# Experts' first block begun in attention's last steps, its weights in eight pieces, and GpSimd in a written order

## The chip, the cores and the metric

The kernel runs on one core of a Trainium2 chip. Its engines are named as the profile names them: PE (TensorE, with PEld for loading weights into it), DVE (VectorE), ACT (ScalarE), POOL (GpSimd) and SP (SyncE); "SPq" and "POOLq" are the DMA queues that SP and GpSimd issue to. The metric is the device time of one execution in microseconds, lower is better. One execution was also profiled; its time and its trace are what lines and intervals are read from.

## The reference

Four images of 32 x 32 tokens with 384 channels go through two layers in 32-bit floats. The part that matters here is the first layer:

```python
# --- layer 0 (metaformer) ---
x = x + _L0_conv_ref(_ln_c(x), ...)      # attention, 12 heads of 32 channels
t = _to_tokens(x)
t = t + _L0_ffn_ref(_ln_t(t), ...)       # four experts, each token goes to two
...
attn = softmax(einsum('bhnd,bhmd->bhnm', q, k) * scale)
attn = attn * final                       # final: row weights x column weights, from groups and a top 96
attn = attn / (attn.sum(axis=2, keepdims=True) + 1e-08)
out = einsum('bhnm,bhmd->bhnd', attn, v)
return out @ proj_w.T
...
scores = einsum('bsd,de->bse', x, gate_w) + gate_b
topk_vals, topk_idx = top_k(softmax(scores), 2)
h = gelu(einsum('bsd,edh->ebsh', x, w1) + b1, approximate=False)
y = einsum('ebsh,ehd->ebsd', h, w2) + b2
out = einsum('bse,ebsd->bsd', masked, y)
```

So each of 1024 tokens per image attends to all the others, column sums of the weighted attention are needed before the values are summed up, and each token is then worked on by the two experts with its highest gate values. The second layer (an outlook attention over 3 x 3 neighbourhoods and a dense layer from a Kronecker product) follows and is not touched.

## The kernel before

**Attention** (`attention`, line 177) runs one main loop (line 882 on) over 202 steps: 4 images x 12 heads = 48 heads, four steps (u = 0 to 3) to a head, two 128-token tiles of keys to a step, and ten more steps at the end in which the last head drains. The variable `step` counts from 0; steps from 192 on have no scores left. In one step, in this order: the scores of the head (PE, line 649) and their exponentials (ACT, line 659); `out`, the weighted values of eight steps before (PE, line 667, into `ps_o`); the softmax's row sums of one step before (PE, line 667, into `ps_z`). At u = 0 the row sums of the head before are gathered (ACT, then SP through a row in DRAM, `z_row`, and back as `zz`), and the next head's `Head` is made: eight small DMAs on GpSimd's queue (lines 636 and 637) that spread its q and k over the partitions. At u = 3 the head that is complete is kept (line 731 on): ACT copies it from PSUM, and SP and GpSimd put it in its place (`q<-po`, GpSimd's two add to what is there). DVE takes the steps `share` of seven steps before (line 711, two passes over 128x1024, then small ones to line 718), at u = 1 `spread` (lines 693 to 699, through `r_row` in DRAM and back as `rz`, broadcast to all partitions), and the preparation of the next image's groups and masks.

The tail of an image lies in the steps of the next: projection and residual (line 766), and then its routing (`routed`, line 793, and `Router`, line 1241), a generator from which the loop takes one portion per step. Routing computes gates and top two on DVE, gives every token a slot in its expert's list, and writes the list to a table in DRAM with 16 scatters per image on GpSimd's queue (line 1400). When the third image's routing is complete, `Router.first` (line 1408) fixes the experts of the first four blocks. It does so before the fourth image's tokens are known; they fill later blocks. The fourth image's projection and routing are done within the experts (`left`, called there `beside`).

**Experts** (`experts`, line 1573) works on 35 blocks of one expert and 256 tokens each: n = 0 to 3 from the first three images, n = 4 to 6 of 128 tokens only, and n = 7 to 34 from all. For a block, GpSimd's queue loads the expert's two weight matrices by an indirect DMA each (`up`, 128x4620 floats, 2.37 MB, and `down`, 128x4992 floats, 2.56 MB, line 1603), the block's slots of the table (`ids`, line 1617) and its tokens (`xb`, line 1627). DVE normalizes the tokens (`norm`, line 1636), PE transposes them (`turn`, line 1646), then twelve `up` chunks of 128 hidden units, six matmuls each (line 1723), with a gelu on ACT (line 1728), then the `down` matmuls: plain ones in blocks 0 and 4 to 6 (line 1747), a form with fewer products and more sums in the others (lines 1767 to 1774). The results go to DRAM by SP (`yg<-y`). In block 0 a portion of `beside` follows each of six chunks. The weights have two buffers (`halves`), so weights of block n+1 are loaded while block n is worked on, each as soon as block n-1 has read it for the last time. When both experts of a tile of 128 tokens have been there, `add` (line 1650) loads the tile's residual `x` by SP, gathers its two results (`yt`, GpSimd, line 1567), adds them (DVE, line 1658) and stores (SP). In the second half of the blocks one tile is added per block.

**Order.** For PE, DVE, ACT and SP the instructions stand in the order in which the program issues them (`tc.manual_schedule`). GpSimd's are placed by the framework's scheduler in this kernel, so that they may run ahead of the program's order, as far as their buffers allow.

Of the kernel before, what the change touches and what calls it, by code (L numbers as in the profile page):

```python
# [10 lines left out]
FP = mybir.dt.float32  # L11
# [165 lines left out]
def attention(net, outer, router, x, x1, unsafe, qkv_wT, gpT, proj_wT, proj_w, gate_w, gate_b):  # L177
# [24 lines left out]
    with ExitStack() as ctx:  # L202

        early = ctx.enter_context(tc.tile_pool(name="at_early", bufs=1))
# [664 lines left out]

        step = -100  # L870
# [18 lines left out]
        for step in range(STEPS + OUT + 2):  # L889
# [13 lines left out]
            if 0 <= step - OUT < STEPS:  # L903
                if (step - OUT) % PAIRS == PAIRS - 1:
                    heads[(step - OUT) // PAIRS].keep()
            b, i = divmod(step, PAIRS * NH)
# [9 lines left out]
            if b and o > 2 * NB:  # L916
                next(routing[b - 1], None)
# [15 lines left out]
            search()  # L933
        residue(B - 1, 0)
# [29 lines left out]
    return left  # L964
# [276 lines left out]
class Router:  # L1241
# [10 lines left out]
    def __init__(self, net, pool, keep, psum):  # L1252
# [34 lines left out]
        self.all = None  # L1287
# [11 lines left out]
        self.weight = [keep.tile([P, NT], FP, name=f"weight_{n}", tag=f"weight_{n}") for n in range(2)]  # L1299
        none = const("none", [P, self.LINE], mybir.dt.int32)  # L1300
# [12 lines left out]
    def route(self, b, logit, mean, rs):  # L1313
# [82 lines left out]
        for t in range(NB):  # L1396
            if t % 2 == 0:
                yield
            for n in range(2):
                s = nc.gpsimd.indirect_dma_start(  # L1400
# [172 lines left out]
def experts(net, router, x1, x2, wup, wdown, beside):  # L1573
# [12 lines left out]
    with ExitStack() as ctx:  # L1586
# [4 lines left out]
        halves = [pool(f"ex_{n}", 1) for n in range(2)]  # L1591
# [3 lines left out]
        def rows(n):  # L1595
            w, t = router.firsts if n < NFIRST else router.all
            return w[:, n : n + 1], t[:, n : n + 1]

        def weights(n):
            up = halves[n % 2].tile([P, KC * HID + NF], FP, name="up", tag="up")  # L1600
            down = halves[n % 2].tile([P, NF * C + C], FP, name="down", tag="down")
            for t, w in ((up, wup), (down, wdown)):
                nc.gpsimd.indirect_dma_start(
                    out=t, out_offset=None, in_=w,
                    in_offset=bass.IndirectOffsetOnAxis(ap=rows(n)[0], axis=0),
                )
            return up, down

        beside = beside(work)
        ids, xbs = {}, {}  # L1610

        def tiles(n):
            return 1 if NFIRST <= n < NLEAD else TT

        def tokens(n):
            t = ids[n] = halves[0].tile([P, TT, router.LINE], I32, name="ids", tag="ids", bufs=6)
            nc.gpsimd.indirect_dma_start(
                out=t[:, : tiles(n), :].rearrange("p t w -> p (t w)"), out_offset=None,
                in_=net.table.rearrange("(r t) w -> r (t w)", t=tiles(n)),
                in_offset=bass.IndirectOffsetOnAxis(ap=rows(n)[1], axis=0),  # L1620
            )

        def fetch(n):
            xb = xbs[n] = halves[n % 2].tile([P, TT, C], FP, name="xb", tag="xb")
            last = (B - 1 if n < NFIRST else B) * NTOK
            for t in range(tiles(n)):
                nc.gpsimd.indirect_dma_start(
                    out=xb[:, t, :], out_offset=None, in_=x1[:last, :],
                    in_offset=bass.IndirectOffsetOnAxis(ap=ids[n][:, t, 0:1], axis=0),
                )  # L1630

        def norm(n):
            xb = xbs[n]
            own = ids.pop(n).bitcast(FP)
            for t in range(tiles(n)):
                nc.vector.tensor_scalar(
                    xb[:, t, :], xb[:, t, :], own[:, t, 1:2], own[:, t, 2:3], ALU.subtract, ALU.mult
                )

        def turn(n):  # L1640
            xb = xbs.pop(n)
            xbT = halves[n % 2].tile([P, KC, XB], FP, name="xbT", tag="xbT")
            for t in range(tiles(n)):
                ps = router.psum()
                for c in range(KC):
                    nc.tensor.transpose(ps[:, c * P : (c + 1) * P], xb[:, t, c * P : (c + 1) * P], net.ident)
                nc.vector.tensor_copy(  # L1647
                    xbT[:, :, t * P : (t + 1) * P], ps[:, :C].rearrange("p (c t) -> p c t", c=KC)
                )
            return xbT  # L1650
# [39 lines left out]
        ws = {0: weights(0)}  # L1690
        for n in range(NFIRST):
            tokens(n)
        fetch(0)
        norm(0)
        xbT = turn(0)
        for n in range(NXB):
# [6 lines left out]
            if n + 1 < NXB:  # L1703
                if n + 1 >= NFIRST:
                    tokens(n + 1)
                ws[n + 1] = weights(n + 1)
                fetch(n + 1)
# [5 lines left out]
            up, down = ws.pop(n)  # L1713
# [5 lines left out]
            for f in (*range(0, 3), *range(6, 9), *range(3, 6), *range(9, 12)):  # L1719
                ps = ps_h.tile([P, XB], FP, name="ps_h", tag="h")[:, :size]  # L1720
                for k in range(KC):
                    o = k * HID + f * P
                    nc.tensor.matmul(  # L1723
                        ps, lhsT=up[:, o : o + P], rhs=xbT[:, k, :size], start=k == 0, stop=k == KC - 1,
                    )
# [57 lines left out]
            if n + 1 < NXB:  # L1783
                xbT = turn(n + 1)
# [684 lines left out]
```

## Time and profile before

| | |
|---|---|
| time, three runs | 2757.79, 2760.5, 2776.32 us; median 2760.5 |
| profiled execution | 2739.55 us; its span 2737.4 us, mean TensorE clock 0.964 |
| busy over the span | PE 2541.4, DVE 1746.2, ACT 1270.0, POOL 635.3 us |
| start to step 0 and the steps of attention | to about 1196 us |
| experts, blocks 0 to 3 | 1198 to 1348 us |
| half blocks, 4 to 6 | 1348 to 1397 us |
| blocks 7 to 34 | 1397 to 2240 us, 29.84 us for an undisturbed one |
| second layer | 2242 to 2737 us |

Busy times are of the profiled execution. In the window lists each engine's busy time is followed by its count of instructions, then the mean granted TensorE clock, the busy share of the core's 16 DMA engines and the rate. In a timeline a line starts with the time from the span's beginning and the duration; what stands in brackets is the idle time of the engine ahead of it and what ended that. `up<-in_wup_dram` means that the tile `up` is written from the DRAM tensor.

### The profile page before, as it was taken

What the parts mean: (1) busy time and instruction counts of PE and PEld (TensorE: products, weight loads), DVE (VectorE), ACT (ScalarE), POOL (GpSimd) and SP (SyncE); (2) the same over time, 40 slices, a digit from 0 to 9 for tenths busy, and PEclk for the clock granted to TensorE, in tenths of its full rate; (3) what the DMA queues carried; (4) which work ended last, traced back from release to release, by engine and by line L of the source; (5) the groups of instructions that cost most, each with busy time, mean ns of one, the idle gap of its engine ahead of it and who ended that gap; (6) DMA issues with size and microseconds to landing.
All of it is one profiled execution on the core that took longest, in us unless ns stands there. A gap on an engine that the chain in (4) does not pass through costs nothing. (4 is left out here: it accounts for less than half of the span.)

```text
span 2737.4 us, 40223 instructions
## 1 busy us (share of the span) xinstructions
PE 2541.4 (93%) x14667; PEld 1549.7 (57%) x14667; DVE 1746.2 (64%) x4490; ACT 1270.0 (46%) x2086; POOL 635.3 (23%) x909
## 2 busy tenths in 40 slices
PE   6979998989899998779999999999999999999988
PEld 3323332333233332248889999999899984555532
DVE  2367768777788778756434454554555468888962
ACT  3768876768677876512122112112111223545455
POOL 2112322252225222613221112222222121210000
PEclk9989999999999998979999999999999999999989
DMA  5133434422332233444574554666566546765532
GB/s 110 38 98 90 105 92 120 106 61 62 83 89 62 62 98 77 138 153 166 214 279 172 202 214 180 219 220 220 197 219 218 213 139 198 224 209 174 181 108 94
DMA packets 189631, 404.14 MB, mean 148 GB/s; under 512 B 83664, under 2 KB 149520, under 8 KB 176368
## 3 DMA queue, kind: packets, MB, share of 16 engines
q0 software_dynamic: 40784, 238.96, 26.5%
q1 hardware_dynamic: 142064, 156.33, 18.3%
q10 hardware_dynamic: 6576, 6.19, 0.8%
q8 instruction: 118, 1.93, 0.3%
q14 instruction: 89, 0.73, 0.1%
HBM read 304.34 MB, written 49.00 MB: 129 GB/s over the span
## 5 line engine op out<-in xcount | busy, mean ns | idle before, releaser
L1728 ACT ACTIVATE h<-ps_h,up 128x256 f32<-128x256 f32 (+1 forms) x420 | 194.8, 464 | 832.2 <-PE ps_h L1723 829.7
L1723 PE MATMUL ps_h<-xbT,up 128*128 128x256 f32 (+1 forms) x2520 | 530.8, 371 | 0.7 <-DVE xbT L1647 0.7
L1723 PEld LDWEIGHTS ps_h<-xbT,up 128*128 128x128 f32 x2520 | 463.3, 191 | 61.7 <-DVE xbT L1647 1.1
L711 DVE CUSTOM_DVE_ANT_0 e<-e,rz,inv 128x1024 f32<-128x1024 f32 x384 | 475.5, 1275 | 17.6 <-DMA rz<-r_row 17.5
L659 ACT ACTIVATE e<-ps_s,ten 128x1024 f32<-128x1024 f32 x384 | 407.1, 1107 | 62.0 <-PE ps_o L667 32.7
L649 PE MATMUL ps_s<-q,k 32*128 32x512 f32 x1536 | 274.3, 663 | 29.1 <-ACT e L659 28.7
L667 PE MATMUL ps_o<-e,wv 128*32 128x512 f32 x1536 | 227.1, 666 | 69.1 <-DVE wv L718 43.9
L636 POOL DMA_DIRECT2D q<-q x192 | 98.2, 512 | 627.9 <-PE ps_s L649 570.5
L667 PE MATMUL ps_z<-e,rt_ones 128*32 128x512 f32 x1536 | 218.8, 642 | 0.0
L391 ACT ACTIVATE below<-tk_left,tk_bound 128x1024 bf16<-128x1024 f32 (+1 forms) x160 | 184.2, 1151 | 63.5 <-DVE tk_bound L397 52.8
L1767 PE MATMUL ps_y<-wsum,hsum 128*128 128x192 f32 x1116 | 197.9, 331 | 10.1 <-DVE hsum L1683 5.9
L1767 PEld LDWEIGHTS ps_y<-wsum,hsum 128*128 128x128 f32 x1116 | 183.7, 192 | 14.3 <-DVE y L1771 7.7
L649 PEld LDWEIGHTS ps_s<-q,k 32*128 32x128 f32 x1536 | 83.0, 188 | 159.6 <-ACT e L659 90.5
L1907 PE MATMUL ps_a<-wa,xnT 128*128 128x486 f32 x384 | 162.3, 572 | 1.8 <-ACT xnT L174 1.8
L1771 DVE TENSOR_TENSOR y<-ps_y,y 128x192 f32<-128x192 f32 x155 | 55.4, 358 | 167.9 <-PE ps_y L1767 164.8
L667 PEld LDWEIGHTS ps_o<-e,wv 128*32 128x32 f32 x1536 | 32.1, 112 | 228.8 <-issue 94.2
L1567 POOL DMA_INDIRECT yt<-yg,index x64 | 78.8, 1232 | 311.4 <-DVE x L1870 148.9
L306 PE MATMUL ps_t<-xnT,wqkv 128*128 128x512 f32 x288 | 136.4, 615 | 3.3 <-ACT xnT L488 2.6
L637 POOL DMA_DIRECT2D k<-k x192 | 126.1, 657 | 9.2 <-issue 6.0
L667 PEld LDWEIGHTS ps_z<-e,rt_ones 128*32 128x32 f32 x1536 | 53.3, 118 | 131.1 <-issue 129.1
L1767 PE MATMUL ps_y<-down,h 128*128 128x192 f32 x744 | 126.0, 326 | 0.0
L1767 PEld LDWEIGHTS ps_y<-down,h 128*128 128x128 f32 x744 | 122.6, 190 | 1.6
(405 smaller groups left out, 3751.1 us busy)
## 6 DMA issues: line engine op xcount, KB each, us to landing
band<-room SPq DMA_DIRECT2D x32, 1560.0 KB
rz<-r_row SPq DMA_DIRECT2D x48, 512.0 KB
yg<-y SPq DMA_DIRECT2D x67, 192.0 KB
q<-q POOLq DMA_DIRECT2D x192, 64.0 KB, 1.9
k<-k POOLq DMA_DIRECT2D x192, 64.0 KB, 2.0
room<-none SPq DMA_DIRECT2D x64, 192.0 KB
x<-x SPq DMA_DIRECT2D x34, 192.0 KB
o<-in_x_dram SPq DMA_DIRECT2D x33, 192.0 KB
```

The costliest lines, as they stand in the source:

```text
L306: nc.tensor.matmul(ps, lhsT=lhsT(k), rhs=rhs(k), start=k == 0, stop=k == KC - 1)
L391: nc.scalar.activation(junk[:n], left[:n], AF.Sign, bias=bound[:n], accum_out=over[:n])
L636: nc.gpsimd.dma_start(out=self.q4[rows_, :], in_=q[:, 512 * half : 512 * half + 512])
L637: nc.gpsimd.dma_start(out=self.k4[rows_, :].rearrange("p (a t) -> p a t", t=P), in_=k[:, :, odd, :])
L649: nc.tensor.matmul(ps[:, half * 512 : half * 512 + 512], lhsT=self.k4[r, u * P : (u + 1) * P], rhs=self.q4[r, :], start=True, stop=True,)
L659: nc.scalar.activation(e, ps, AF.Exp, bias=shift, scale=QK_SCALE)
L667: nc.tensor.matmul(ps[r : r + 32, :], lhsT=lhsT(odd), rhs=self.es[2 * u + odd][:, half * 512 : half * 512 + 512], start=u == 0, stop=u == ...
L711: nc.vector.tensor_tensor_reduce(self.es[m], self.es[m], self.rz, 1.0, self.im["inv"][:, m, self.h : self.h + 1], ALU.mult, ALU.add, self. ...
L1723: nc.tensor.matmul(ps, lhsT=up[:, o : o + P], rhs=xbT[:, k, :size], start=k == 0, stop=k == KC - 1,)
L1728: nc.scalar.activation(hs[f // 3][:, f % 3, :size], ps, AF.Gelu, bias=up[:, KC * HID + f : KC * HID + f + 1])
L1767: nc.tensor.matmul(ps, lhsT=left[f], rhs=right[:, f, :], start=f == 0, stop=f == HF - 1)
L1907: nc.tensor.matmul(pa[:, :HW_], lhsT=xnTs[i][:, k, :], rhs=wa[:, k, hh * HW_ : (hh + 1) * HW_], start=k == 0, stop=k == KC - 1,)
```

## The change

GpSimd is added to the engines whose order is the program's. What the scheduler did is thereby replaced by the order of the calls: in experts, for block n+1 of the first four `xb` and then `up` and `down`; for the later ones `ids`, `up`, `down`, `xb`; and `yt` of a tile after these.

The functions of a block become a class, `Blocks`, made while attention still runs. For this the tiles of the pool `at_early`, which attention needs for its preparation only, go to the other side of the memory, and are given back at the step at which `Router.first` is done; the first block's buffers take that place. So that this comes sooner, the third image's routing takes two portions per step. From the order of instructions in the changed kernel: `first` is done in step 178 (before: 185). That step issues the four `ids`; each of steps 179 to 186 issues one piece of the first weights (four of `up`, 0.59 MB each, four of `down`, 0.64 MB), the first of them the two `xb` as well. At step 188 comes the norm, at step 189 the transposes, with copies by ACT instead of DVE. Steps 192 to 199 take one and two chunks of `up` and gelu by turns, in PSUM tiles of the scores and SBUF tiles of q, both free by then. In experts block 0 has only its `down` matmuls left, and `beside` is called after every fourth. On GpSimd the 16 scatters of the third image stand together, ahead of the `ids`, the weights and the loads of head 46; and a memset of one column, `spacer`, stands ahead of every scatter.

```diff
-        early = ctx.enter_context(tc.tile_pool(name="at_early", bufs=1))
+        soon = ctx.enter_context(ExitStack())
+        early = soon.enter_context(tc.tile_pool(name="at_early", bufs=1, side="right"))
...
+        def chunks():
+
+            cols, h = [], None
+            for f in range(NF):
+                if f % 4 == 0:
+                    h = lasting.tile([P, NTOK], FP, name="q", tag="q", bufs=6)
+                if f % 2 == 0:
+                    ps = ps_s.tile([P, NTOK], FP, name="ps_s", tag="s")
+                p = ps[:, f % 2 * 512 : f % 2 * 512 + XB]
+                blocks.up(0, f, blocks.xbT, p, XB)
+                col = h[:, f % 4 * XB : f % 4 * XB + XB]
+                blocks.gelu(0, f, p, col)
+                cols.append(col)
+                yield
+            blocks.cols = cols
...
+            if step >= STEPS:
+                if step == STEPS:
+                    upward = chunks()
+                for _ in range(1 + step % 2):
+                    next(upward, None)
...
             if b and o > 2 * NB:
-                next(routing[b - 1], None)
+                for _ in range(2 if b == B - 1 else 1):
+                    next(routing[b - 1], None)
+            if blocks is None and router.firsts is not None:
+                assert pending == [None, None] and begun == len(tiles)
+                soon.close()
+                pool = outer.enter_context(tc.tile_pool(name="ex_0", bufs=1, side="right", reuse_waits="tile"))
+                blocks = Blocks(net, router, x1, wup, wdown, pool)
+                known = step
+                for one in range(NFIRST):
+                    blocks.tokens(one)
+                weighing = blocks.weigh(0, 4)
+            if blocks and step == known + 1:
+                blocks.fetch(0)
+            if blocks and step > known:
+                next(weighing, None)
+            if step == STEPS - 4:
+                blocks.norm(0)
+            if step == STEPS - 3:
+                blocks.xbT = blocks.turn(0, nc.scalar.copy)
...
             for n in range(2):
+                nc.gpsimd.memset(self.spacer, 0.0)
                 s = nc.gpsimd.indirect_dma_start(
...
+    def weigh(self, n, pieces):
+        self.ws[n] = []
+        row = at = self.rows(n)[0]
+        if pieces > 1:
+            at = self.router.pool.tile([P, pieces], mybir.dt.int32, name="rows_piece")
+            for i in range(pieces):
+                self.nc.vector.tensor_scalar(
+                    at[:, i : i + 1], row, float(pieces), float(i), ALU.mult, ALU.add
+                )
+        for name, w in (("up", self.wup), ("down", self.wdown)):
+            t = self.halves[n % 2].tile([P, w.shape[-1]], FP, name=name, tag=name)
+            self.ws[n].append(t)
+            size = w.shape[-1] // pieces
+            for i in range(pieces):
+                cols = slice(i * size, (i + 1) * size)
+                self.nc.gpsimd.indirect_dma_start(
+                    out=t[:, cols], out_offset=None, in_=w.rearrange("r (i c) -> (r i) c", i=pieces),
+                    in_offset=bass.IndirectOffsetOnAxis(ap=at[:, i : i + 1], axis=0),
+                )
+                yield
...
         for n in range(NXB):
...
             if n + 1 < NXB:
                 if n + 1 >= NFIRST:
-                    tokens(n + 1)
-                ws[n + 1] = weights(n + 1)
-                fetch(n + 1)
+                    blocks.tokens(n + 1)
+                for ask in (blocks.fetch, blocks.weights)[:: 1 if n + 1 < NFIRST else -1]:
+                    ask(n + 1)
...
-            for f in (*range(0, 3), *range(6, 9), *range(3, 6), *range(9, 12)):
+            early = n == 0 and blocks.cols is not None
+            for f in () if early else (*range(0, 3), *range(6, 9), *range(3, 6), *range(9, 12)):
...
+                        h = blocks.cols[f] if early else hs[f // 3][:, f % 3, :]
                         nc.tensor.matmul(
-                            ps, lhsT=hs[f // 3][:, f % 3, t * P : (t + 1) * P], rhs=down[:, f * C : (f + 1) * C],
+                            ps, lhsT=h[:, t * P : (t + 1) * P], rhs=down[:, f * C : (f + 1) * C],
                             start=f == 0, stop=f == NF - 1,
                         )
+                        if early and f % 4 == 3:
+                            next(beside, None)
...
-        with tc.manual_schedule(engines={eng.PE, eng.DVE, eng.Activation, eng.SP}):
-            left = attention(
+        with tc.manual_schedule(engines={eng.PE, eng.DVE, eng.Activation, eng.SP, eng.Pool}):
+            left, blocks = attention(
```

## The prediction

> **What bounds the kernel now.** I began with the page's busy shares, then read windows stage by stage, because the share is an average over stages with different limits.
>
> ```profile
> PE 2541.4 (93%) x14667; PEld 1549.7 (57%) x14667; DVE 1746.2 (64%) x4490; ACT 1270.0 (46%) x2086; POOL 635.3 (23%) x909
> ...
> PE   6979998989899998779999999999999999999988
> ```
>
> PE is busy nearly everywhere; the only long dip is the two 7s in the middle, where attention ends. Windows around it (columns: window, length, busy us and count of PE, PEld, DVE, ACT, POOL, clock, DMA share, GB/s):
>
> ```profile
> 1130.00:1150.00 20.00, 14.51 (x96) 3.95 (x88) 15.90 (x51) 9.52 (x11) 17.15 (x20) 0.91 0.63 200
> 1150.00:1170.00 20.00, 11.96 (x78) 3.36 (x80) 10.49 (x23) 7.05 (x7) 5.25 (x6) 0.87 0.55 181
> 1170.00:1200.00 30.00, 16.38 (x76) 4.29 (x69) 21.33 (x56) 3.04 (x4) 3.17 (x4) 0.61 0.19 43
> 1200.00:1245.00 45.00, 45.00 (x166) 31.51 (x165) 11.16 (x31) 5.68 (x12) 9.16 (x11) 0.97 0.71 252
> ```
>
> From 1150 to 1200 PE works 28.3 of 50 us; from 1200 (experts) it never stops. So matmuls moved ahead of 1200 can be hidden, and anything that makes PE wait later is paid in full. The waits of DVE from 1130 to 1196 (waiting engine and line, releaser, total, times, longest):
>
> ```profile
> DVE zall L693 <- DMA zz<-z_row: 8.3, 2, 6.2
> DVE e L711 <- DMA rz<-r_row: 7.5, 3, 2.9
> ```
>
> These are the small round trips through DRAM (`z_row`, `r_row`) that each head makes. The 6.2 ends at 1158.7, two waits of 2.9 at 1143.6 and 1164.9: beside the two weight loads of 4.9 MB issued at 1141. GpSimd's timeline shows what leads up to them (start, duration, then the instruction):
>
> ```profile
> 1099.57 0.53 POOL L636 DMA_DIRECT2D q<-q  x1 [11.05 <-PE ps_s L649]
> ...
> 1110.27 2.51 POOL L1400 DMA_INDIRECT table<-rt_ge,rt_there  x1 [3.39 <-issue]
> ...
> 1134.77 0.57 POOL L636 DMA_DIRECT2D q<-q  x1
> ...
> 1141.06 1.03 POOL L1603 DMA_INDIRECT up<-in_wup_dram,rows_w_first  x1 [0.30 <-DVE wv L718]
> 1142.39 0.98 POOL L1603 DMA_INDIRECT down<-in_wdown_dram,rows_w_first  x1 [0.30 <-issue]
> ...
> 1157.77 0.95 POOL L1627 DMA_INDIRECT xb<-x,ids  x1 [7.88 <-DMA ids<-table,rows_t_first]
> ```
>
> The 16 scatters (1110.27 to 1134.77, 24.5 us) lie between two heads' q/k loads, and `ids` lands late behind the weights. Then block 0 on PE:
>
> ```profile
> 1198.45 11.24 PE L1723 MATMUL ps_h<-xbT,up 128*128 128x256 f32 x42 [0.65 <-DVE xbT L1647]
> 1209.53 2.12 PE L306 MATMUL ps_t<-wproj,q 128*128 128x388 f32 x6
> ...
> 1227.73 7.90 PE L1747 MATMUL ps_y<-down,h 128*128 128x384 f32 x24
> ...
> 1243.87 1.46 PE L1723 MATMUL ps_h<-xbT,up 128*128 128x256 f32 x6
> ```
>
> **The change part by part.** All sums are against the profiled execution, 2739.55 us (span 2737.4 and 2.2 around it). The median of the runs is 2760.5, 21 us above; I carry the difference over to it.
>
> 1. Block 0's up phase moves. It takes 1198.45 to 1227.73 = 29.3 us, of which six projections take 6 x 1.95 = 11.7 and stay; 17.6 us of up matmuls leave. With them goes the gap from the last `out` (1195.34) to 1198.45, the norm and turn of the block: 3.1. Against it: steps 198 and 199 issue chunks after the last `out` (2 x 1.3 = +2.6), and projection 0, now after four down matmuls (1.3 us), needs the last head's `q<-po` pair. ACT copies po about 1 us after the last `out`, and the accumulating load took 3.5 us to land beside 1.7 of issue: about 6 to 7.5 us after the last `out`, against about 4 when PE comes to it: +3 to +4. Sum -17.6 - 3.1 + 2.6 + 3.6 = **-14** (from -20 to -8). The 12 gelus (0.46 us each) and the transposes go to ACT, busy 3 of 30 us there, and PE. The norm (2 x 0.47) goes to DVE, the busy engine of that stretch: 1 us, counted in part 3.
>
> 2. Heads' loads behind the scatters. In the written order the 16 scatters, contiguous (1.27 us pitch from the trace and 16 memsets of about 0.1), then four `ids`, the first of which waits for the last scatter to land (3.4), then a `q<-po` pair (1.7), two `xb` (2.5) and weight piece 1 (1.3) all stand ahead of head 46's loads. Routing runs twice as fast, so the scatters start about the time they become ready, some 9 us earlier: about 1101 + 26 + 2.3 + 5.3 + 1.7 + 2.5 + 1.3 = 1140, less what is ready sooner; 8 loads land at 1136 to 1139 where step 184 began at 1124.5 (with first()'s 5.2 us of DVE now ahead of it: 1127 to 1130). PE waits: **+8** (3 to 15; queued behind it are the scores, so exps, totals and shares too). Before, head 46's loads went out at 1099.57, ahead of all scatters, and cost nothing.
>
> 3. The burst is cut. Eight pieces of about 0.6 MB, one per step, replace 4.9 MB at once. 6.2 + 2.9 us of DVE waits would go: **-9** (0 to -12). What is late next is the same chain at its plain length: two waits of 2.05 and 1.73 us remain at 1175.9 and 1181.5 with DMA at 0.19, so nothing more is won there. The added norm, piece-row arithmetic and transposes: +1.
>
> The Trainium skill ("DMA: Bandwidth & Descriptors", Queues, rings and completion order) says that each DMA engine goes round the queue rows it has work for, packet by packet. By that rule SP's small round trips should only have taken turns with the burst, pieces would change nothing, and the sum would be 9 us higher; the row above shows 6.2 us beside the burst against 2.05 without, so I let the row decide.
>
> 4. Half blocks (n = 4 to 6), order on GpSimd. Before, xb ran ahead of the down weights:
>
> ```profile
> 1359.43 0.95 POOL L1627 DMA_INDIRECT xb<-x,ids  x1 [0.30 <-issue]
> 1360.68 0.95 POOL L1627 DMA_INDIRECT xb<-x,ids  x1 [0.30 <-issue]
> 1365.94 0.94 POOL L1603 DMA_INDIRECT down<-in_wdown_dram,rows_w_all  x1 [4.31 <-DVE y L1752]
> ```
>
> After, xb(n+1) follows down(n+1), which waits for the block before to end. xb(6) is issued at 1367.2 and lands 9.5 later (the median behind down) at 1376.7; its norm is due at 1373.1, the end of block 5's up phase: +3.6 and the norm and turn, about +4.5. xb(7) the same, +4.5 to 5.5; xb(5) lands at 1355 for 1356: +0.5. The transposes stand ahead of the down matmuls on PE, so all of it shows: **+10** (4 to 12). In whole blocks xb is due some 15 us into the block and a landing at +8 is early.
>
> 5. The adds. In the 17 blocks from n = 18 that add a tile of results, the gathers `yt` left the scheduler 10 us into the block before, when DMA was quiet:
>
> ```profile
> 2130.67 1.20 POOL L1567 DMA_INDIRECT yt<-yg,index  x1 [10.97 <-DVE x L1658]
> ```
>
> In the written order they come after up, down and xb, into the burst (down goes out 4.1 us before the block starts, yt about at its start). The add is already late from another load:
>
> ```profile
>   DMA x<-x: 60.3, 8
> ```
>
> The add started 8.4 to 9.4 us into most blocks, and the block's period was 29.84 plus what exceeds 8.4 (9.20 gave 30.63; 11.10 gave 32.54): 7.7 us lost over 16 blocks. With yt landing at +8.9 to +9.4, each loses 0.5 to 1.0: 8 to 16 instead of 7.7, so **+5** (-2, if x stays the later one; up to +22 if yt lands at +10.3).
>
> 6. The rest of the written order. `q<-po` ahead of all eight loads of the next head puts them 1.7 us later: loads would end 10.75 us after the last scores and land at 12.7, where four steps of 3.32 are 13.3; it is covered by 0.6 us, and if not costs a fraction of a us in each of some 46 heads. In images 0 and 1 the scatters go out in two groups instead of one: 0, from -3 to +5. 64 memsets on GpSimd (23% busy) cost nothing but the delay in part 2.
>
> Sum: -14 + 8 - 9 + 1 + 10 + 5 + 0 = **+1 us**: 2740.6 profiled, **2762** by the median.
>
> **The rivals.**
>
> A, the order costs nothing: xb and yt are hidden, since x is the later load anyway and xb(6) lands sooner than the median. Then -14 + 8 - 9 + 1 = -14; with the heads' loads hidden as well, -22: 2738 to 2747. For it speaks that x ends those waits, not yt; against it that yt moves into the stretch in which x itself takes 9 us.
>
> B, slower: the transfers behind the weights. Price: yt at +10.3 costs 22 instead of 5, half blocks 12, heads' loads 15, with the block's -14 and the burst's -9: +1 + 17 + 2 + 7 = +27, 2788. It decides from the point where the add starts more than 9.5 us into its block. For it: xb, issued in that place, took 8.0 to 10.8 us; against: yt is small and x goes on SP's queue.
>
> C, the tail of attention is TensorE's: moved, not hidden. In 1170 to 1196 the clock was 0.63. There eight `out` matmuls take 1.93 us against 1.07 at full clock, and one and a half chunks twice 1.95 = 3.9: 5.8 us a step against the 4.6 that the last steps took: eight steps cost +10, 2772. The skill ("TensorE: Matmul & The Clock Gate", What's actually happening) says that the clock falls back when TensorE idles and is full again after a busy stretch of about 3.4 us; by that rule the chunks would themselves lift it, a step would take 3.1 us, and the tail would not be TensorE's. The trace's 1200 to 1245 at 0.97 agrees.
>
> D, it doesn't do what it says: one piece per step is the order in the program, but GpSimd comes to it 10 to 20 us late behind scatters and waits, so that pieces go out back to back and the burst stays: +9 on the sum, 2771.
>
> **How the numbers follow.** Forecast 0.42, A 0.18, B 0.17, C 0.10, D 0.13. One per cent is 27.6 us, about what a measurement of this kernel can tell from no change. Only B's upper half with another mishap passes it upward, and A only with the full block gain (-20) and burst (-12); but the terms' ends add up beyond them both ways (+40 with all upper ends and block 0 at -8), so I say faster 0.11, within 0.72, slower 0.17. Range: from A's lower half, -22 (2738), to B with one term at its end, +29 (2790).
>
> **What would show it.** Part 1: block 1's up matmuls start some 34 us after the last `out` instead of 48.5, with PE idle before projection 0 on `q<-po`. Part 2: PE waits before the scores of head 46 for the DMAs of q and k. Part 3: the 6.2 us wait for zz is gone. Part 4: DVE's norm of xb waits on DMA in blocks 5 and 6. Part 5: the adds wait for yt, not x, and periods are near 30.5. Wrong it would be above all if yt or xb land at another place in the burst than the rows say, or if the scatters' end moves.

## The result, and the profile after

The changed kernel takes 2806.88 us in the median (2799.90 to 2816.14), the kernel before 2759.14 beside it: a ratio of 1.0155, interval 1.0126 to 1.0183. It is slower by 43 to 48 us where +1 was forecast, and lies above the range. In a later session, on chip 1 (the chip of the first is not on record), the kernel before took 2742 and the changed one 2806 (ratio 1.0230, 1.0208 to 1.0252). So a run is given below with its ratio to the kernel before of its own session.

The page of the changed kernel, busy shares and the PE row of the slices:

```profile
PE 2569.4 (91%) x14667; PEld 1558.9 (55%) x14667; DVE 1745.3 (62%) x4492; ACT 1271.1 (45%) x2088; POOL 641.1 (23%) x979
...
PE   6979998989898997689889999999999999999988
```

The dip in the middle was to be filled; it has become deeper and longer. Windows of the changed kernel over it (same columns as before):

```profile
1130.00:1150.00 20.00, 7.78 (x28) 1.98 (x32) 10.50 (x44) 5.25 (x7) 12.76 (x19) 0.53 0.03 6
1150.00:1170.00 20.00, 14.79 (x107) 4.36 (x102) 13.70 (x38) 10.83 (x12) 12.89 (x15) 0.93 0.53 131
1170.00:1200.00 30.00, 20.18 (x112) 5.41 (x113) 14.86 (x35) 10.97 (x11) 13.84 (x18) 0.73 0.63 190
1200.00:1245.00 45.00, 39.89 (x230) 17.84 (x223) 32.13 (x78) 17.75 (x26) 3.10 (x4) 0.93 0.16 38
```

From 1130 to 1150 PE works 7.8 of 20 us with DMA at 0.03: hardly any bytes move there. From 1200 to 1245 the chunks do fill PE (39.9 of 45 us, clock 0.93), as intended. DVE's waits from 1100 to 1250:

```profile
DVE e L712 <- DMA rz<-r_row: 17.6, 4, 7.6
DVE rt_start L1471 <- issue: 13.0, 1, 13.0
DVE zall L694 <- DMA zz<-z_row: 11.5, 4, 6.9
```

The first and third are the round trips that the pieces were to shorten: 29.1 us from head 42's row sums to the last `out`. Over the same stretch the three traces of the kernel before have 17.3, 21.6 and 16.7 us, and a repeat of the changed kernel 19.9. They vary much, but are not shorter. The second is new, and GpSimd's timeline shows what it is:

```profile
1117.65 1.03 POOL L1445 DMA_INDIRECT table<-rt_ge,rt_there  x1 [0.20 <-POOL rt_spacer L1444]
...
1137.29 0.97 POOL L1445 DMA_INDIRECT table<-rt_ge,rt_there  x1 [0.19 <-issue]
1138.25 0.12 POOL L1467 MEMSET rt_begun<- 128x4 f32 x1
1138.29 0.11 POOL L1469 MEMSET rt_start<- 128x1 f32 x1
1142.99 1.79 POOL L1664 DMA_INDIRECT ids<-table,rows_t_first  x1 [4.59 <-DVE rows_t_first L1516]
...
1155.37 1.05 POOL L1674 DMA_INDIRECT xb<-x,ids  x1 [0.30 <-issue]
...
1160.00 1.70 POOL L1645 DMA_INDIRECT up<-in_wup_dram,rows_piece  x1 [0.30 <-DVE rr L696]
1161.69 0.58 POOL L637 DMA_DIRECT2D q<-q  x1
```

`Router.first` clears two corners of small tiles with memsets of 0.1 us on GpSimd. In the written order they stand behind 16 scatters, so DVE reaches `rt_start` at 1138.44 after 13.00 us of idleness; DVE's `share` of the heads stands behind it, and PE's `out` behind that:

```profile
1145.70 1.93 PE L668 MATMUL ps_o<-e,wv 128*32 128x512 f32 x8 [9.59 <-DVE tk_parts L396]
```

On GpSimd then come ids, xb and a piece, and only then head 46's loads, at 1161.7, where head 46's scores wait:

```profile
1169.26 3.21 PE L650 MATMUL ps_s<-q,k 32*128 32x512 f32 x8 [3.28 <-DMA k<-k]
```

Where the time went, stage by stage, read from the traces base2 and again, taken in one session (marks: the copy of a head's row sums on ACT, heads counted from 0; the norm of a block's tokens on DVE). The last two columns give the same difference between the changed kernel's first trace and base, which are of two sessions with the kernel before at 2759 and 2763 us, and what the prediction had:

| stage | before, us | changed, us | difference | first trace | predicted |
|---|---|---|---|---|---|
| start to row sums of head 42 | 1066.0 | 1085.3 | +19.3 | +6.3 | 0 |
| heads 42 to 47 | 104.9 | 123.3 | +18.4 | +17.4 | +8 - 9 + 1 |
| head 47 to norm of block 4 | 164.7 | 162.1 | -2.6 | +1.5 | -14 |
| blocks 4 to 8 (half blocks) | 79.1 | 93.4 | +14.3 | +13.0 | +10 |
| blocks 8 to 34 (adds) | 782.5 | 798.5 | +16.0 | +13.7 | +5 |
| rest | 539.2 | 539.1 | -0.1 | -0.6 | 0 |
| span | 2736.4 | 2801.7 | +65.3 | +51.3 | +1 |

No stage that the change touches is better than forecast, and the first two, whose terms summed to nothing, lost 37.7 us between these two traces.

### The profile page after: what moved, and what is told of

The parts are those of the page before. It is cut to its first block, busy times and chain, and to the rows that moved or that the text cites. A ratio compares the mean times of both kernels' runs of the same rounds, so it can differ in the third digit from the quotient of the medians.

```text
span 2814.4 us, 40249 instructions
## 1 busy us (share of the span) xinstructions
PE 2569.4 (91%) x14667; PEld 1558.9 (55%) x14667; DVE 1745.3 (62%) x4492; ACT 1271.1 (45%) x2088; POOL 641.1 (23%) x979
## 5 line engine op out<-in xcount | busy, mean ns | idle before, releaser
L1717 ACT ACTIVATE h<-ps_h,up 128x256 f32<-128x256 f32 (+1 forms) x408 | 188.5, 464 | 863.7 <-PE ps_h L1711 851.3
L1711 PE MATMUL ps_h<-xbT,up 128*128 128x256 f32 (+1 forms) x2448 | 515.6, 371 | 8.3 <-ACT h L1717 7.6
L1711 PEld LDWEIGHTS ps_h<-xbT,up 128*128 128x128 f32 x2448 | 449.2, 191 | 67.6 <-ACT h L1717 8.6
L650 PE MATMUL ps_s<-q,k 32*128 32x512 f32 x1536 | 282.0, 678 | 42.0 <-ACT e L660 35.0
L739 POOL DMA_DIRECT2D q<-po x96 | 77.9, 907 | 740.8 <-DMA q<-po 485.9
L637 POOL DMA_DIRECT2D q<-q x192 | 162.3, 846 | 99.3 <-PE ps_s L650 67.9
L638 POOL DMA_DIRECT2D k<-k x192 | 168.9, 885 | 12.1 <-ACT k L551 7.0
L1645 POOL DMA_INDIRECT up<-in_wup_dram,rows_w_all x31 | 37.4, 1206 | 403.9 <-ACT h L1717 403.6
```

The lines of the kernel that those rows point to most:

```text
L637: nc.gpsimd.dma_start(out=self.q4[rows_, :], in_=q[:, 512 * half : 512 * half + 512])
L638: nc.gpsimd.dma_start(out=self.k4[rows_, :].rearrange("p (a t) -> p a t", t=P), in_=k[:, :, odd, :])
L650: nc.tensor.matmul(ps[:, half * 512 : half * 512 + 512], lhsT=self.k4[r, u * P : (u + 1) * P], rhs=self.q4[r, :], start=True, stop=True,)
L1711: self.nc.tensor.matmul(ps, lhsT=up[:, o : o + P], rhs=xbT[:, k, :size], start=k == 0, stop=k == KC - 1,)
L1717: self.nc.scalar.activation(out, ps, AF.Gelu, bias=up[:, KC * HID + f : KC * HID + f + 1])
```

## The experiments

**The same kernels again.** base and base2 are the kernel before and again is the changed kernel, each on the chip of the runs beside it.

> The kernel before, unchanged, profiled once more, to see how far one profiled execution of it stands from another: the profiled one on record took 2739.55 us where the runs' median is 2759. If the first 42 heads of attention take as long as in that profile (the sums of heads copied 1068.9 us after the start), then the 23.5 us which the changed kernel is later by head 42 are the change's; if they take 10 to 20 us longer, most of them are chance.

> The kernel before, profiled on the chip of the runs beside it. The median of its runs was 2762.6 us on one chip and 2741.4 on another. If its first 42 heads take 1086 us here with a median near 2762, and 1069 with one near 2741, what differs between chips is a stage of attention that the change doesn't touch on purpose.

base: one execution of 2765 us, head 42 at 1086.0; base2: 2738.5 us, head 42 at 1066.0. So the 20 us between the two levels of the kernel before do lie in attention, mostly around heads 21 and 33, where routing's scatters run. In the changed kernel head 42 came at 1092 in the first trace and at 1085 in the repeat: what the change costs in attention depends on which level of the kernel before it is held against.

> The changed kernel, unchanged, beside the next two on one chip. Theory of the parts: 2800 to 2810 wherever it runs, 1.5 to 2.4 per cent above the kernel before.

again: 2805.6 us, 1.0230 of the kernel before (1.0208 to 1.0252), as expected.

**The written order without the early block, and the early block without the written order.**

```diff
# order_alone: blocks made in experts, one portion of routing per step
-            if blocks is None and router.firsts is not None:
+            if False:
...
# free
-        with tc.manual_schedule(engines={eng.PE, eng.DVE, eng.Activation, eng.SP, eng.Pool}):
+        with tc.manual_schedule(engines={eng.PE, eng.DVE, eng.Activation, eng.SP}):
             left, blocks = attention(
```

> The changed kernel without the early block: GpSimd in the written order with the spacers, but block 0 begun in experts, its weights in two loads, routing one portion per step. Theory W (the written order is the loss, the early block itself gains some 8 us): slower than before by 35 to 50 us, 2795 to 2810. Theory E (the early block is the loss): only the half blocks' 13 and the adds' 12 us remain, 2780 to 2785.

> The changed kernel with GpSimd's instructions placed by the scheduler again, as before the change; all else as changed. Theory W: as fast as before or faster, 2740 to 2765. Theory E: still some 25 us slower than before, 2780 to 2790.

order_alone: 2828.0 us, 1.0241 (1.0221 to 1.0261). free: 2771.2 us, 1.0041 (1.0021 to 1.0062). So the order is the loss, as theory W had it, but larger than W expected, since without the early block something new is late. PE's longest wait of order_alone at the start of experts:

```profile
PE ps_t L1685 <- DVE xb L1675: 25.8, 2, 25.4
```

The first weights, ids and xb go out where the program names them, at 1232 behind the last head, while the scheduler had sent them 74 us earlier (at 1158 in base). The early block repairs this, and is worth some 21 us within the written order (2828 to 2807, in two sessions; 24 by the ratios); under the scheduler, which needs no such repair, it is no gain at all: 2771.2 us lies 6 us above the upper end that W gave.

**The memsets.**

```diff
-        nc.gpsimd.memset(self.begun[:, 0, :], 0.0)
+        nc.vector.memset(self.begun[:, 0, :], 0.0)
```

(and the three others in `first` and `schedule`)

> The changed kernel with one edit: the four memsets of one or four columns in Router.first and Router.schedule go to DVE instead of GpSimd. Theory W (in the written order they stand behind 16 scatters, and DVE, PE and ACT wait for them): the idle 13.0 us of DVE before rt_start at 1138 go, and some 6 us of PE's stall in block 2, together 15 to 20 us, about 2788. Theory E (the tail of attention is late from routing at double rate and from the weights' pieces whatever GpSimd does): a few us at most, above 2800.

memsets: 2809.0 us, 1.0157 (1.0128 to 1.0187): nothing gained, theory W's number fails. The 13.0 us are gone from DVE's waits, but zz and rz now stand for 32.9 us in place of 29.1 (one trace each), and head 46's loads, which start at 1153.5 instead of 1161.7, still bind the tail (PE waits 5.2 us there for k, 3.3 in the changed kernel). The wait was real and had another one right behind it.

**The tail's order.**

```diff
-                for _ in range(2 if b == B - 1 else 1):
+                for _ in range(2 if b == B - 1 and i < 32 else 1):
```

> The changed kernel, but the third image's routing runs at two portions per step for five steps only and then at one, so that its scatters are spread four to a step and head 46's q and k loads stand ahead of the ids, xb and weights (first done in step 180 instead of 178). Theory L (head 46's loads stand behind 16 scatters, ids, xb and a piece, and bind the tail from then on; the memsets' 13 us lay beside this): the tail between heads 42 and 47 gives back 12 to 17 us, 2790 to 2795. Rival P (the pieces themselves keep z_row's and r_row's round trips at 5 to 7 us): the waits for zz and rz stay, at most 5 us, above 2802.

tail: 2802.7 us, 1.0221 (1.0198 to 1.0244), against 1.0230 for the changed kernel on that chip: no gain that can be told from none. Its trace gives back 3.5 us between heads 42 and 47 (119.8 us where again has 123.3) and the memsets' wait is still there (10.9 us). Only with both edits, as in mended, does that stage fall to 107.5 us, 2.6 above the kernel before; the other edits in mended alone leave it at 124.1 (xb_first) and 123.3 (yt_ahead). Each wait hid the other.

**xb and yt in experts.**

```diff
# xb_first
-                for ask in (blocks.fetch, blocks.weights)[:: 1 if n + 1 < NFIRST else -1]:
+                for ask in (blocks.fetch, blocks.weights):
# yt_ahead: at the top of a block, ahead of ids and weights
+                take(soon_)
```

> The changed kernel, but for every block GpSimd asks for xb ahead of up and down, where the changed kernel does so for the first four only. Theory Q (a half block ends before its successor's xb, queued behind down, has landed): blocks 5 and 6 lose their 5 and 7.5 us, 2794, and periods of whole blocks stay as they are. Rival (xb then waits for ids with the weights queued behind it, and the weights are late): whole blocks longer than 29.85 us, above 2807.

> The changed kernel, but GpSimd gathers the two yt of an add one block earlier in the written order, ahead of the next block's ids and weights, as the scheduler had it. Theory Y (the adds are late because yt queues behind up, down and xb): the last 16 block periods, which sum to 13.7 us more than in the kernel before, return to its 30.3 us each, total 2793 to 2796. Rival X (the residual x, which SP loads beside the same weights, is as late): periods stay near 31.1, 2805 to 2809.

xb_first: 2777.1 us, 1.0130 (1.0106 to 1.0155), 28 us below the changed kernel there: more than the half blocks. They lose nothing now, as theory Q had it, and the stage of the adds, blocks 8 to 34, is 2.0 us longer than in base2 where the repeat of the changed kernel is 16. What DVE's adds wait for, in the changed kernel and in xb_first (16 adds each):

```profile
  DMA x<-x: 144.8, 16
```

```profile
  DMA x<-x: 127.4, 16
```

9.05 and 7.96 us each; the kernel before has 8.00, 7.88 and 7.81 in its three traces, the repeat of the changed one 8.82. The profile names SP's x as the load that ends the wait in all of them, not yt. In best4, where the landing of the second yt is on record for some blocks, it stands 1 us ahead of the add; in the changed kernel it is not on record. By this reading x lands some 1 us later when GpSimd's queue holds up, down, xb and yt at once. yt_ahead: 2806.9 us, 1.0235 (1.0206 to 1.0264), no gain. Inside an image its block periods are those of the kernel before (blocks 18 to 24 take 182.2 us, in base2 183.0), so taking yt out of the burst helps as taking xb out does; but at the first add of each image my edit makes yt wait for the results just stored, with the next weights queued behind it (37.7 us of GpSimd's idleness at 1997), and blocks 25 to 27 lose 8 us; blocks 8 to 17, with the first of these adds, lose 6.5.

**All together.**

```diff
-                o = late[0].tile([P, C], FP, name="o", tag="o", bufs=2)
+                o = late[0].tile([P, C], FP, name="o", tag="o", bufs=4)
```

> The changed kernel with the edits of memsets, yt_ahead, xb_first and tail together, and four buffers instead of two for the fourth image's residuals in experts, whose loads in block 0 wait for the store of the tile two before (PE stands 7.5 us for it). If the parts add up: 2807 - 13 - 13 - 14 - 6 (memsets in block 2) - 7 = 2754, 5 to 10 us less than the kernel before. If they lie beside one another or turn into other waits: 2765 to 2780.

> The changed kernel with the edits of memsets, xb_first and tail, and four buffers for residuals, but yt gathered where the changed kernel does. In xb_first the adds were no longer late (periods 1.2 us longer in sum than before, not 13.7), in mended the earlier gathers cost 8 us where an image's last block ends. So: mended less 7 us, 2758 to 2762, against 2768 for mended; 40 to 45 us below the changed kernel, and at or 5 us below the kernel before on a chip where that takes 2762. If xb_first's adds were recovered by chance: as mended, 2768.

> As best, and SP asks for the fourth image's residuals 1 to 3 ahead of block 0 and then four tiles ahead, instead of one. Theory R (PE's 7 us stall in block 0 is a residual that is loaded one tile ahead, beside three blocks' weights): 5 to 7 us less than best, 2752 to 2756. Rival (projection 3 waits for the store of tile 1, or the loads just land together): the same as best.

mended: 2768.5 us, 1.0099 (1.0080 to 1.0118). best, without yt_ahead: 2755.3 us, 1.0050 (1.0033 to 1.0066), as expected, 50 us below the changed kernel. The four buffers didn't help: PE still stood 7.0 us in block 0. best2 asks for the residuals four ahead: 2753.3 us, 1.0044 (1.0026 to 1.0063). In its trace that stall is 0.5 us, but PE waits 7.7 us in block 1 for a gelu instead, which stands behind the fourth image's routing on ACT, and the difference to best is within the error. How the stall looked in the changed kernel, on DVE and on PE:

```profile
1267.58 0.55 DVE L783 TENSOR_TENSOR o<-o,ps_t 128x384 f32<-128x384 f32 x1 [10.17 <-DMA o<-in_x_dram]
```

```profile
1260.38 0.49 PE L1693 MATMUL ps_t<-ident,xb 128*128 128x128 f32 x3
1268.36 0.87 PE L1693 MATMUL ps_t<-ident,xb 128*128 128x128 f32 x3 [7.48 <-DVE gate_o L784]
...
1283.68 1.46 PE L1711 MATMUL ps_h<-xbT,up 128*128 128x256 f32 x6
```

A residual that is loaded one tile ahead (issued at 1253.7) takes over 10 us beside xb(1), up(1), down(1), xb(2) and up(2): block 0's `up` buffer is free before experts begin, so block 2's weights start as well.

**The order in attention.**

```diff
# best3: in route, the iota of the list four portions earlier, where its tile is free
         nc.vector.tensor_reduce(sel, ge, AX.X, ALU.add)
+        ids = self.temp("ge", [P, NB, self.LINE], mybir.dt.int32)
+        nc.gpsimd.iota(ids, pattern=[[P, NB], [0, self.LINE]], base=b * NTOK, channel_multiplier=1)
# best4, also: in keep, and emitted after heads.append(Head(n + 1))
-                            nc.gpsimd.dma_start(out=there, in_=po[r : r + 32, :], accum_op=ALU.add)
+                            adds.append((there, po[r : r + 32, :]))
```

> best2, with the iota of each routing's list moved four portions earlier in the program, to where its tile is free, so that GpSimd has done it before the loads of the next head stand ahead of it. Theory I (DVE waits 2 to 3 us in each routing for the iota behind q<-po and eight loads): 4 to 8 us less than best2, mostly between heads 30 and 35, 2745 to 2749 on a chip where that took 2753. Rival (DVE has slack there): the same as best2, 2751 to 2755.

> best3, and GpSimd's pair q<-po of a finished head is asked for after the loads of the next head's q and k instead of ahead of them. Theory K (the loads wait for the copy and for SP's pair in front of them, late by 4 to 6 us in every head, which shows in the heads with little other work for PE): 4 to 8 us less than best3. Rival (the loads land in time anyway, four steps ahead): as best3 within 2 us.

best3: 2758.1 us, 1.0031 (1.0017 to 1.0044); best2 had 1.0044 on the same chip in another session, so a gain isn't certain by time. In the traces the waits for the iota, 6.8 us in two of them between 560 and 1000 us in best2, are gone, and head 34 is 4.4 us earlier than in best2. In the repeat of the changed kernel one of these waits was (the profile names the memset that follows the iota, at 869.01 behind 868.80):

```profile
869.60 0.17 DVE L1438 COPY rt_ge<-mv 128x8 f32<-128x8 f32 x1 [3.18 <-POOL rt_spacer L1444]
```

best4: 2746.1 us, 0.9987 (0.9970 to 1.0004), best3 beside it 2758.1. The intervals don't touch, so the order of `q<-po` against the next head's loads matters; the size is uncertain, since the two traces show 4.0 us of it by head 41 and the tails of these two executions differ the other way.

**The two disputed terms by themselves**, both against best4.

```diff
# whole
-                weighing = blocks.weigh(0, 4)
+                weighing = blocks.weigh(0, 1)
# nochunks: the loop of twelve up chunks runs in experts again
-                    upward = chunks()
```

> best4, but the first block's weights in two loads instead of eight, one per step. Theory of the prediction (the burst makes z_row's and r_row's round trips wait 6.2 and 2.9 us, pieces avoid it): 5 to 9 us slower than best4. Rival D (the same bytes go in the same few steps, and the round trips wait for them all the same, 4.0 to 6.5 us as in mended): within 3 us of best4.

> best4, but block 0's twelve up chunks and gelus stand in experts again; its weights, norm and transposes stay in attention's tail. Theory of the prediction's part 1 (the chunks fill PE's idle time in the tail; 17.6 us leave block 0, 2.6 come back behind the last out, and projection 0 waits 3.6): slower than best4 by 10 to 15 us. Rival (block 0 without its chunks has its projections too close for the residuals and the weights of the blocks behind, which takes most of it back): slower by 3 to 8 us.

whole: 1.0007 (0.9996 to 1.0019), 3.4 us above best4, with intervals that overlap. The waits in the tail, best4 first, then whole:

```profile
DVE e L712 <- DMA rz<-r_row: 12.5, 3, 9.1
DVE zall L694 <- DMA zz<-z_row: 11.5, 4, 5.4
```

```profile
DVE zall L694 <- DMA zz<-z_row: 13.0, 4, 10.1
DVE e L712 <- DMA rz<-r_row: 7.2, 3, 3.6
```

24.0 us with eight pieces, 20.2 with two loads: no shortening by the pieces is seen. By time they are worth 3.4 us in the median, which can't be told from nothing; the 5 to 9 of the prediction's theory are not reached. nochunks: 2755.2 us, 1.0024 (1.0009 to 1.0039), 9.1 us above best4: between the prediction's 10 and the rival's 8.

**The early block under the scheduler, mended.**

> free, on the chip of the run beside it. On the first chip it took 1.0041 of the kernel before, which there took 2762. Theory M (the written order's 47 to 65 us and nothing else differ from chip to chip, since the kernel before is what varies): 1.004 to 1.012 of the kernel before here too, whichever chip it is.

> free (GpSimd placed by the scheduler), with two of the mended parts: the third image's routing at two portions for five steps only (the edit of tail), and the residuals four ahead (the edit of best2). Theory V (the early block is worth 9 to 14 us, and free lost it to head 46's loads behind 16 scatters and to a 9.5 us stall for residuals in block 0): 10 to 17 us less than free, at or 5 us below the kernel before. Rival (the tail binds on z_row's and r_row's round trips whatever comes before): 4 to 7 us less than free, above the kernel before.

free_again: 1.0011 (0.9996 to 1.0026) on a chip where the kernel before took 2774.6; theory M's 1.004 to 1.012 fails, and the early block under the scheduler is at most a small loss. free2, with the edits of tail and best2: 2773.0 us, 0.9981 (0.9963 to 0.9998), 3.8 us less than free_again in the median (8 by the ratios) where 10 to 17 were expected. The stall for residuals in block 0 (9.5 us in free) is 0.5 there, and zz and rz hold DVE for 26.6 us in the tail: the rival's reading is nearer, though the rival had it above the kernel before. It is the only version whose interval lies below the kernel before, and only just: by 0.2 per cent.

## Why the prediction was wrong

In short: the two halves of the sum failed in different ways. The gains that carried it, the block's -14 and the burst's -9, did not come; of the losses, the half blocks, the adds and the heads' loads were in their places and larger, and the rest of the written order, put at 0, was not 0.

**Part 6, "the rest of the written order: 0, from -3 to +5".** Before head 42 the changed kernel lost 6 us in its first trace and 19 in the repeat. I had seen that `q<-po` moves ahead of the loads and called it covered by 0.6 us; best4 shows that it isn't. The iota, on which DVE waits up to 3.7 us in the routings, I didn't list among GpSimd's instructions at all. With both edits (best4) head 42 comes 10.0 of these 19.3 us earlier. The other 9.3 stay open, and 4.5 of them are there before head 0. Nor can the 6 us be put on the written order: free, without it, has 4.9 of them.

**Part 2, "+8 (3 to 15)".** The place was right: head 46's loads behind scatters, ids, xb and piece 1, seen as PE's wait for k, though that is only 3.3 us and 1.2 in the repeat. But I counted on GpSimd's queue only DMAs. Two memsets of 0.1 us in `first`, which the scheduler had run at the start of the kernel, went behind the scatters too, and cost DVE 13.0 us; the repeat shows what PE lost by it, where base2 has 5.1:

```profile
PE ps_o L668 <- DVE tk_parts L396: 22.5, 2, 16.7
```

The 13 us lay largely beside the loads' lateness, so that neither memsets nor tail alone gained. Two more memsets in `schedule` cost less. PE's wait for `hsum` in the same stretch is 8.6 us in the repeat, 8.5 in tail, 5.5 in best with the memsets moved, and 5.2 in base2: some 3 us at most. The first trace has another wait there, 6.9 us for a gelu in block 2; it is still 6.2 us in memsets, so the memsets are not its cause, which stays open.

**Part 3, "-9 (0 to -12)".** The step that failed is the inference from the burst to its pieces. SP issues the read-back `zz` when `z_row` has landed. Where little moves, the two stand 1.7 us apart; beside the first weights they stand 6.1 apart in the kernel before, 6.2 in the changed one, and 8.9 in whole:

```profile
1149.45 0.53 SPq L683 DMA_DIRECT2D z_row<-zr  x1
1155.55 0.37 SPq L685 DMA_DIRECT2D zz<-z_row  x1
1172.32 0.53 SPq L683 DMA_DIRECT2D z_row<-zr  x1
1174.03 0.38 SPq L685 DMA_DIRECT2D zz<-z_row  x1
```

```profile
1176.61 0.53 SPq L684 DMA_DIRECT2D z_row<-zr  x1
1182.85 0.37 SPq L686 DMA_DIRECT2D zz<-z_row  x1
```

```profile
1144.72 0.53 SPq L684 DMA_DIRECT2D z_row<-zr  x1
1153.65 0.38 SPq L686 DMA_DIRECT2D zz<-z_row  x1
```

So one round trip was indeed late beside the weights, and it was so with pieces too: the same bytes go by. It is not always so: base has 2.2 us there and the repeat of the changed kernel 2.4. One row each, 6.2 against 2.05, was too little to cost 9 us by; and of the two waits of 2.9, the one that ended at 1143.6 had begun before the weights were issued at 1141.06. The Trainium skill ("DMA: Bandwidth & Descriptors", Queues, rings and completion order) says that the queues take turns packet by packet; the prediction read from it that pieces change nothing, and no run here shows a change by them. Rival D came true in its price: the gain of 9 did not come. Its mechanism is seen in part: after piece 1 at 1160 three pieces left between 1167.4 and 1171.3, since GpSimd came late to them.

**Part 1, "-14 (-8 to -20)".** From the last `out` to block 1's first up matmul the kernel before takes 48.5 us and the changed one 41.2, where the prediction's sign was 34. Projection 0's wait for `q<-po` is not seen (PE goes from the down matmuls into it at 1249.4), but 7.5 us are lost four matmul groups later on a residual. I had asked what the projections lose as cover for one of their inputs, `q`, and not for the other. Once the residuals are asked for early, in best2 and best4, that stretch is 32.8 us, 15.7 less than before: the size was right. But then blocks 1 to 3 take 101 to 102 us to the norm of block 4 where the kernel before took 92.9, with PE's 8 us wait for a gelu among it; so the stage from head 47 to block 4, which in the changed kernel gained 2.6 us or lost 1.5, gains about 7 there. By time the chunks are worth 9.1 us in a mended kernel.

**Part 4, "+10 (4 to 12)".** Right in mechanism, +13.0 and +14.3 in size. PE's waits for xb's norm were forecast at 0.5, 4.5 and 5.5; their visible idle times in the changed kernel are 0.74, 3.53 and 3.74 (ahead of blocks 5, 6 and 7; the first was 0.75 before the change), and after the last two the next matmuls run slower (24 down matmuls in 9.6 and 10.3 us at a granted clock of 0.83 and 0.77, against 7.9 at 1.00 before), which I left out:

```profile
1427.04 0.52 PE L1693 MATMUL ps_t<-ident,xb 128*128 128x128 f32 x3 [3.53 <-DVE xb L1683]
1427.40 9.60 PE L1836 MATMUL ps_y<-down,h 128*128 128x384 f32 x24
```

**Part 5, "+5 (-2 to 22)".** The size lay within its bounds, at +13.7 and +16.0, but by luck, for the reason was off: by the profile it is not yt that lands last but x, held back by all that GpSimd has in flight.

Rival B came nearest, with 2788: slower, by transfers behind the weights. It named the half blocks, the adds and the heads' loads, and these stages did lose 44 us by the first trace. What carried the time out of the range was the burst's -9 and the block's -14, which B kept, and in the repeat the 19 us before head 42 as well. Rival C did not happen: eight `out` matmuls took 1.06 us beside the chunks.

## What to carry to other kernels

When an engine that a scheduler placed is put into the program's order, list every instruction that this engine has, the 0.1 us ones first, and ask for each who waits for it and what now stands ahead of it; here two memsets held VectorE for 13.0 us and two iotas for 6.8. A scheduler's order also contains prefetches that the program doesn't spell out (weights 74 us ahead, xb ahead of the down weights, yt into the quiet half), and each must be written down or is lost. Work moved under cover also was cover: ask for all the inputs of what stays behind. And before a wait is costed from one row, look at the same row in a second trace.

## What the runs showed that I had not expected

- The kernel before took 2741 to 2748 us in three sessions, 2759 and 2763 in two and 2775 in one, by the chip and the session; the changed kernel took 2807 and 2806 in its two. Between the two traces of the kernel before, the 20 us lie in attention's scatter stretches. Why is open.
- A small load on SP's queue is later the more GpSimd has in flight: DVE's wait for x averaged 7.96 us with yt alone in the burst and 9.05 with xb as well.
- An idle PE costs more than the idle time: after waits of 3.5 us the same 24 matmuls took 9.6 us at a granted clock of 0.83, instead of 7.9 at 1.00.
- A scatter of 128 rows holds GpSimd for 1.27 us from one to the next with or without a memset between, 16 of them for 20.6 us in the changed kernel and 24.5 before, and everything of the engine's behind them waits.
